# A deferred queue of small VectorE steps in an attention stage: weights, due steps, and the shift transposes one task step sooner

## The chip, the cores and the metric

The kernel runs on one core of one Trainium2 chip. The metric is the device time in microseconds (us) of one execution; lower is better. The core's engines each work through their own list of instructions in order and meet at semaphores: TensorE (PE in the profile, its weight loads PEld), VectorE (DVE), ScalarE (ACT), GpSimd (POOL), and SyncE (SP), which issues most DMAs.

## The reference

Two transformer layers on x of shape (2, 1024, 512), float32. Each layer is `x = x + layernorm(attn(layernorm(x)))` and then `x = x + layernorm(ffn(layernorm(x)))`. The first attention is a softmax over heads for every position on its own; the first feed-forward uses weights rounded to -1, 0, 1. The part that matters here is the second layer's attention, 16 query heads over 4 key heads of width 32, causal:

```
q, k, v = rope(x @ q_w.T), rope(k), v        # k, v from x @ kv_w.T
logits  = einsum('bhqd,bhkd->bhqk', q, k_ctx) / sqrt(32) + causal mask
probs   = softmax(logits, axis=-1)
out     = einsum('bhqk,bhkd->bhqd', probs, v_ctx)   # then @ c_w.T
```

The second feed-forward keeps the two largest of every four hidden values. Only the attention stage, from about 438 to 916 us of the profiled span, is touched by the change; the instructions of the other stages keep their order.

## The kernel before

The attention is cut into 16 tasks. A task is one batch b (0, 1), one block Q of 512 queries (0, 1) and one key head g (0 to 3), with the 4 query heads that share it; tiles carry these three numbers, so `mxs_0_1_2` belongs to batch 0, Q 1, g 2, which is task number 6 (`tk.n` runs 0 to 15 in that order). Each task is done twice over.

The first pass finds the softmax shift. `score_step` (L689 to L714) takes one tile of 128 queries and one chunk of up to 512 keys: for each head TensorE writes the scores into a PSUM bank (`psc`), VectorE takes the row maximum (`mxs`, L710), and ScalarE exponentiates in place and adds up the row (`psc`, L712, and `sms`). The bank is free once ScalarE is done with it. `shifts` (L974) then turns the maxima and sums into one number per row, maximum plus logarithm of the sum. For Q 1 it first merges two chunks: `mfin` and `md` on VectorE, an exponential of `md` on ScalarE (L986), then `md` times `sms` and `sfin` on VectorE. `minus_log` follows (tiles `lge` to `lgw`) and `in_pieces` splits the shift into three bf16 pieces in `pm0` or `pm1`. That is 23 small steps for Q 1, 18 for Q 0.

The second pass needs the shift along the other axis. `maxima_T` (L993) calls `pieces_T`: four TensorE transposes of the pieces (`pmt`, L927) into a bank and a VectorE copy to SBUF (`mT`, L929). `prob_step` then computes transposed scores (`pst`, L1004), adds the shift with a matmul against ones (`pst<-mT,onesb`, L1011), and ScalarE exponentiates into `pT` (L1017); `value_step` multiplies with v (`po`, L1033). Banks for `psc`, `pst`, `pmt`, projections and outputs come from one function, `ring`, which hands out seven PSUM banks in turn.

The main loop (L1283 on) runs over `t_steps`, one task step per 128 keys of a task's second pass. In each it issues a `prob_step`, then score steps of later tasks as far as `wanted(step)` asks (a step without any is called idle here), then some queued VectorE steps, then whatever `later` has put down for this step number. Projections of the second batch (`pq`, `pkv`, `ra` and `rbq`, `pkT`, `pqT`) and output products (`py`) are spread over the steps in this way.

The small VectorE steps are not issued where they are written. `shift_drops` and `norm_drops` are lists of calls: the first holds the shift steps, the second the inverse root (`nv_y`, `ny_y`, `rs_y`) and the four normalisations (`tmpy`, L237) of an output block. `drip(n)` takes n entries, shifts first. It is called with 2 after each row maximum, with 2 at the end of a step with scores and with 8 at the end of an idle step. Behind the exponential, `shifts` puts six empty entries, so that VectorE's next entry comes later than ScalarE's work. `apply` adds each normalised block to x on GpSimd (`x_sb`, L1063), which also finishes the rotations `ra` (L635).

```
shift_drops.items.append(lambda: nc.scalar.activation(d, d, AF.Exp))
shift_drops.items += [None] * 6
...
later(first[tk.n] - 1, [lambda: maxima_T(tk)])
...
n_drops = 2 if pos > before else 8
in_order(lambda: drip(n_drops))
```

`maxima_T` empties `shift_drops` first if anything is left. The order on VectorE is otherwise partly the scheduler's: in the built program the queued steps stand one after each maximum and the rest behind the last maximum of the step.

Of the kernel before, what the change touches and what calls it, by code (L numbers as in the profile page):

```python
# [13 lines left out]
AF = mybir.ActivationFunctionType  # L14
# [10 lines left out]
def two_layer_sandwich(  # L25
# [22 lines left out]
    nc = tc.nc  # L48
# [129 lines left out]
    class Drops:  # L178
# [1 line left out]
            self.items = []  # L180

        def __getattr__(self, op):
            return lambda *a, **kw: self.items.append(lambda: getattr(nc.vector, op)(*a, **kw))

        def drain(self, n=None):
            while self.items and n != 0:
                f = self.items.pop(0)
                if f is not None:
                    f()
                n = None if n is None else n - 1  # L190

    shift_drops, norm_drops = Drops(), Drops()

    def in_order(f):
        with tc.manual_schedule(engines={mybir.EngineType.DVE}):
            f()

    def drip(n):
        for _ in range(n):
            (shift_drops if shift_drops.items else norm_drops).drain(1)  # L200

    def ln_stats(pool, srcs, name, roots=True, st=None, vec=None):

# [32 lines left out]
    def ln_apply(dst, src, mv, rs, k, vec=None):  # L236
        (vec or nc.vector).tensor_scalar(  # L237
            dst, src, mv[:, k, 0:1], rs[:, k : k + 1], ALU.subtract, ALU.mult
        )
# [424 lines left out]
    for b in range(B):  # L664
        for Q in range(NQ):
            for g in range(NKV):
                tk = Task()
# [48 lines left out]
    with tc.manual_schedule(engines={mybir.EngineType.PE, mybir.EngineType.Pool}):  # L716
# [69 lines left out]
        for g in range(NG):  # L786
            nxt = None
            for hc in range(HC):
# [7 lines left out]
                if g == NG - 1 and hc == HC - 1:  # L796
                    tk = tasks[0]
# [38 lines left out]
                else:  # L836
# [10 lines left out]
                    elif hc == 2 * GT:  # L847
# [5 lines left out]
                        tk = tasks[0]  # L853
# [7 lines left out]
                step = HC * g + hc  # L861
# [49 lines left out]
    def in_pieces(m, name):  # L911

        nonlocal n_pm
        pm = pms[n_pm % 2]
        n_pm += 1
        r1 = s1.tile([P, GT, REP], F32, tag="r1", name=f"r1_{name}", bufs=1)
        shift_drops.tensor_copy(pm[:, :, :, 0], m)
        shift_drops.tensor_tensor(r1, m, pm[:, :, :, 0], ALU.subtract)
        shift_drops.tensor_copy(pm[:, :, :, 1], r1)
        shift_drops.tensor_tensor(pm[:, :, :, 2], r1, pm[:, :, :, 1], ALU.subtract)  # L920
        return pm
# [23 lines left out]
    def minus_log(v, m, name):  # L945


        def tmp(tag, dtype=F32):
            t = small_tile(tag, f"{tag}_{name}", dtype)
            return t.rearrange("p n k -> p (n k)")[:, : GT * REP].rearrange("p (i r) -> p i r", i=GT)  # L950

        vi = v.bitcast(I32)
        e, f = tmp("lge", I32), tmp("lgf", I32)
        ef, z, z2, p = tmp("lgw"), tmp("lgz"), tmp("lgy"), tmp("lgp")
        shift_drops.tensor_scalar(e, vi, 23, None, ALU.logical_shift_right)
        shift_drops.tensor_scalar(
            f, vi, 0x7FFFFF, 0x3F800000, ALU.bitwise_and, ALU.bitwise_or
        )
        fr = f.bitcast(F32)
        shift_drops.tensor_scalar(ef, e, -LN2, 126.5 * LN2, ALU.mult, ALU.add)  # L960
        shift_drops.tensor_scalar(z, fr, R2, None, ALU.add)
        shift_drops.reciprocal(z, z)
        shift_drops.scalar_tensor_tensor(z, fr, R2, z, ALU.subtract, ALU.mult)
        shift_drops.tensor_tensor(z2, z, z, ALU.mult)
        shift_drops.tensor_scalar(p, z2, 1.0 / 9.0, 1.0 / 7.0, ALU.mult, ALU.add)
        shift_drops.tensor_tensor(p, p, z2, ALU.mult)
        shift_drops.scalar_tensor_tensor(p, p, 1.0 / 5.0, z2, ALU.add, ALU.mult)
        shift_drops.scalar_tensor_tensor(p, p, 1.0 / 3.0, z2, ALU.add, ALU.mult)
        shift_drops.scalar_tensor_tensor(p, p, 1.0, z, ALU.add, ALU.mult)
        shift_drops.scalar_tensor_tensor(ef, p, -2.0, ef, ALU.mult, ALU.add)  # L970
        shift_drops.tensor_tensor(ef, ef, m, ALU.add)
        return ef

    def shifts(tk):  # L974

        in_order(shift_drops.drain)
        m, sm = tk.mx[:, :, :, 0], tk.sm[:, :, :, 0]
        if tk.Q > 0:
            n = tk.Q + 1
            m = s1.tile([P, GT, REP], F32, tag="mfin", name=f"mfin_{tk.nm}")  # L980
            shift_drops.tensor_reduce(m, tk.mx[:, :, :, :n], AX.X, ALU.min)
            d = s1.tile([P, GT, REP, n], F32, tag="md", name=f"md_{tk.nm}", bufs=1)
            shift_drops.tensor_tensor(
                d, m.unsqueeze(3).to_broadcast([P, GT, REP, n]), tk.mx[:, :, :, :n], ALU.subtract
            )
            shift_drops.items.append(lambda: nc.scalar.activation(d, d, AF.Exp))  # L986
            shift_drops.items += [None] * 6
            shift_drops.tensor_tensor(d, d, tk.sm[:, :, :, :n], ALU.mult)
            sm = s1.tile([P, GT, REP], F32, tag="sfin", name=f"sfin_{tk.nm}")
            shift_drops.tensor_reduce(sm, d, AX.X, ALU.add)  # L990
        tk.pm = in_pieces(minus_log(sm, m, tk.nm), tk.nm)

    def maxima_T(tk):  # L993
        in_order(shift_drops.drain)
        tk.mT = pieces_T(tk.pm, tk.nm)
# [47 lines left out]
    def output_parts(st, Q):  # L1043


        nm = f"y_{st.b}_{Q}"
        alone = st.b == B - 1 and Q == NQ - 1
        n = 1 if alone else GT
        ys = {}

        def y_of(ii):
            tag = "xn" if alone or ii == 0 else f"y{ii}"
            return s1.tile([P, D], F32, tag=tag, name=f"tmp{nm}_{ii}", bufs=1)

        def add(tiles, mv, ys):
            in_order(norm_drops.drain)
            vec = nc.vector if alone else norm_drops
            rs = inverse_root(s1, mv, n, f"{nm}_{tiles[0]}", vec=vec)

            def apply(k, ii):  # L1060
                ln_apply(ys[ii], py_of.pop(ii) if alone else ys[ii], mv, rs, k)
                xt = x_sb[:, st.b * TB + GT * Q + ii, :]
                soon(lambda: nc.gpsimd.tensor_tensor(xt, xt, ys[ii], ALU.add))  # L1063

            for k, ii in enumerate(tiles):
                if alone:
                    apply(k, ii)
                else:
                    norm_drops.items.append(lambda k=k, ii=ii: apply(k, ii))

        py_of, got = {}, []

        def part(ii):
            py = py_of[ii] = ring(f"p{nm}_{ii}")
            for c in range(DC):
                nc.tensor.matmul(  # L1076
                    py, st.oT[Q][:, c, ii * P : (ii + 1) * P], wc1[:, c, :],
                    start=(c == 0), stop=(c == DC - 1),
                )
            if ii == 0:  # L1080
                in_order(norm_drops.drain)
            ys[ii] = y_of(ii)
            if not got or alone:
                got[:] = [
                    s1.tile([P, n, 6], F32, tag=f"st_y{n}", name=f"st_{nm}_{ii}", bufs=1),
                    s1.tile([P, n, 2], F32, tag=f"mv_y{n}", name=f"mv_{nm}_{ii}", bufs=2),
                ]
            stats, mv = got
            k = 0 if alone else ii
            if not alone:  # L1090
                nc.vector.tensor_copy(ys[ii], py)
            nc.vector.bn_stats(out=stats[:, k, :], in_=py if alone else ys[ii])
            nc.vector.bn_aggr(out=mv[:, k, :], in_=stats[:, k, :])
            if alone:
                add([ii], mv, ys)

        parts = [lambda ii=ii: part(ii) for ii in range(GT)]
        return parts if alone else parts + [lambda: add(list(range(GT)), got[1], ys)]
# [6 lines left out]
    def later(step, parts, apart=1):  # L1105
        for k, f in enumerate(parts):
            due.setdefault(step + k * apart, []).append(f)
# [47 lines left out]
    with tc.manual_schedule(engines={mybir.EngineType.PE, mybir.EngineType.Pool}):  # L1155
# [2 lines left out]
            for tk in tasks for ii in range(GT) for ch in range(tk.Q + 1)  # L1158
        ]
        t_steps = [(tk, j) for tk in tasks for j in range(GT * tk.Q + GT)]  # L1160
        first, s_end, n = {}, {}, 0
        for tk in tasks:
            first[tk.n] = n
            n += GT * (tk.Q + 1)
# [1 line left out]
        pos = s_end[0]  # L1166

        def scored(tk):
            shifts(tk)
            later(first[tk.n] - 1, [lambda: maxima_T(tk)])  # L1170

        def scores_up_to(n, step, between=lambda: None):
            nonlocal pos
# [109 lines left out]
        for step, (tk, j) in enumerate(t_steps):  # L1283
            hold_adds[0] = True
            prob_step(tk, j)
            flush()
            prev.append((tk, j))

            waiting = [lambda: values(step)]

            def between():
                while waiting:
                    waiting.pop()()

            before = pos
            scores_up_to(wanted(step), step, between)
            between()
            n_drops = 2 if pos > before else 8
            in_order(lambda: drip(n_drops))
            for f in due.pop(step, []):  # L1300
                f()
        values(len(t_steps))
# [2 lines left out]
        while due:  # L1305
            step = min(due)
# [429 lines left out]
```

## Time and profile before

| | us |
|---|---|
| median of 3 runs | 1532.32 |
| the runs | 1530.01, 1533.43, 1532.32 |
| profiled execution, its own time | 1527.97 |
| profiled execution, span of its instructions | 1526.3 |
| TensorE busy | 1459.2 |
| VectorE busy | 1008.3 |
| ScalarE busy | 728.0 |
| GpSimd busy | 319.7 |

The profile is of one execution, 4.35 us shorter than the median of the timed runs, and 1.67 us of its time lie around the span. Busy times are sums over the whole span. A busy matmul can also be one that runs at a lower clock, so the granted clock has to be read beside it: its mean is 0.979 over the span, and the lower stretches are short and lie mostly in the attention stage.

### The profile page before, as it was taken

The page shows a single profiled execution, that of the slowest core. Times are in us where ns is not written, and L with a number is a line of the kernel's source. Part 1 is how long each engine was busy: PE and PEld are TensorE (multiplying, and loading weights), DVE is VectorE, ACT ScalarE, POOL GpSimd, SP SyncE. Part 2 cuts the span into 40 slices and gives each one's busy share as a digit, 9 for nine tenths or more (in the row PEclk, how much of TensorE's full clock was granted, in tenths as well). Part 3 has the DMA queues.
Part 4 walks back from the last instruction along what each step waited for, and adds up shares of the span by engine and source line. Part 5 has one row for each costly group of instructions (what it writes and reads, how often), then busy time and mean ns, then how long its engine had stood idle before and what let it go on. Part 6 is the DMA issues. An engine that isn't in the chain of part 4 may idle for free.

```text
span 1526.3 us, 20269 instructions
## 1 busy us (share of the span) xinstructions
PE 1459.2 (96%) x6998; PEld 1046.4 (69%) x6998; DVE 1008.3 (66%) x2315; ACT 728.0 (48%) x1847; POOL 319.7 (21%) x424
## 2 busy tenths in 40 slices
PE   7999999999889898999999999999999999999997
PEld 4558887767655454445444447888888888888886
DVE  6976465652577768657876645784688468846773
ACT  4243343322477656688886982450345034404420
POOL 1105475332222314323432011000200020001001
PEclk9999999999989999999999999999999999999998
DMA  7200211201474433343640003533452345235312
GB/s 296 76 14 28 83 56 42 56 18 53 107 176 108 118 100 90 102 127 92 175 135 1 1 1 145 205 133 145 171 195 97 145 172 201 92 149 212 147 49 76
DMA packets 78871, 167.52 MB, mean 110 GB/s; under 512 B 10224, under 2 KB 35824, under 8 KB 76720
## 3 DMA queue, kind: packets, MB, share of 16 engines
q1 hardware_dynamic: 72928, 148.39, 30.1%
q0 software_dynamic: 4784, 16.52, 2.8%
q10 hardware_dynamic: 1056, 1.31, 0.3%
q8 instruction: 55, 0.90, 0.2%
q14 instruction: 48, 0.39, 0.1%
HBM read 138.94 MB, written 27.26 MB: 109 GB/s over the span
## 4 chain that ended last, share of the span: by engine, by line
PE 80%; DVE 9%; ACT 6%; issue 2%; POOL 1%; DMA 1%; SPq 0%; DVEq 0%; ACTq 0%; POOLq 0%
PE acc L1496 13%; PE ph L409 9%; PE pb_u L1345 7%; PE pb_g L1345 7%; PE po L428 5%; PE py L1076 4%; PE pst L1004 4%; PE pq L286 4%; PE psc L698 4%; PE pc_u L1345 4%; PE pc_g L1345 4%; PE pq L603 4%; ACT psc L712 4%; PE po L1033 3%; DVE mxs L710 3%; PE pa_u L1345 2%
## 5 line engine op out<-in xcount | busy, mean ns | idle before, releaser
L710 DVE TENSOR_REDUCE mxs<-psc 128x1 f32<-128x512 f32 (+3 forms) x384 | 199.8, 550 | 70.7 <-PE psc L704 36.0
L712 ACT ACTIVATE psc<-psc,mxs 128x512 f32<-128x512 f32 (+3 forms) x384 | 217.5, 601 | 24.0 <-DVE mxs L710 18.1
L1017 ACT ACTIVATE pT<-pst 128x512 f32<-128x512 f32 (+3 forms) x384 | 160.2, 548 | 87.4 <-PE pst L1011 87.0
L409 PE MATMUL ph<-xTg,w 128*128 128x512 f32 x704 | 171.9, 397 | 1.7 <-DVE xTg L399 0.9
L409 PEld LDWEIGHTS ph<-xTg,w 128*128 128x128 f32 x704 | 132.1, 189 | 31.5 <-DVE xTg L399 1.2
L1549 POOL TENSOR_TENSOR x_sb<-x_sb,o 128x512 f32<-128x512 f32 x14 | 19.1, 1363 | 549.4 <-DVE o L237 549.2
L1496 PE MATMUL acc<-wd,h 128*128 128x256 f32 x512 | 121.6, 379 | 0.0
L1019 POOL TENSOR_SCALAR_AFFINE_SELECT pT<-pT 128x256 f32<-128x256 f32 x128 | 52.0, 413 | 309.3 <-ACT pT L1017 305.8
L1496 PEld LDWEIGHTS acc<-wd,h 128*128 128x128 f32 x512 | 97.0, 190 | 13.1
L712 ACT ACTIVATION_READ_ACCUMULATOR psc<-psc,mxs 128x1 f32 x384 | 96.0, 251 | 0.0
L1033 PE MATMUL po<-pT,v 128*32 128x512 f32 (+3 forms) x768 | 92.7, 520 | 1.5 <-POOL pT L1019 1.1
L1496 PE MATMUL acc<-wd,hx 128*128 128x256 f32 x384 | 93.3, 379 | 0.0
L698 PE MATMUL psc<-k,q 128*128 128x512 f32 (+3 forms) x256 | 90.9, 425 | 1.7 <-ACT psc L712 0.7
L418 POOL TENSOR_TENSOR hl<-h,hl 128x512 fp32r<-128x512 f32 x44 | 57.1, 1302 | 159.2 <-ACT hl L417 159.1
L428 PE MATMUL po<-w,hl 128*128 128x512 f32 x352 | 88.3, 393 | 0.4 <-DVE tmp L237 0.4
L1004 PE MATMUL pst<-q,k 128*128 128x512 f32 (+3 forms) x256 | 76.7, 394 | 11.5 <-ACT psc L712 10.8
L415 DVE TENSOR_TENSOR h<-h,ph 128x512 f32<-128x512 f32 x44 | 30.0, 684 | 83.9 <-PE ph L409 73.9
L1496 PEld LDWEIGHTS acc<-wd,hx 128*128 128x128 f32 x384 | 73.0, 190 | 9.9
L1406 DVE TENSOR_TENSOR gate<-gate,ab 128x1024 f32<-128x1024 f32 x32 | 39.2, 1225 | 59.2 <-ACT ab L1403 59.2
L698 PEld LDWEIGHTS psc<-k,q 128*128 128x128 f32 x256 | 49.0, 200 | 42.6 <-ACT pT L1017 18.6
L1513 ACT COPY p<-acc 128x512 f32<-128x512 f32 x8 | 4.7, 583 | 152.2 <-PE acc L1496 152.2
L428 PEld LDWEIGHTS po<-w,hl 128*128 128x128 f32 x352 | 65.7, 188 | 15.5 <-DVE tmp L237 1.3
(304 smaller groups left out, 3002.9 us busy)
## 6 DMA issues: line engine op xcount, KB each, us to landing
w<-kept SPq DMA_DIRECT2D x64, 512.0 KB, 5.8
wd<-keptd SPq DMA_DIRECT2D x16, 1024.0 KB, 7.8
q<-dq SPq DMA_DIRECT2D x60, 256.0 KB, 5.0
w<-in_f_wg SPq DMA_DIRECT2D x32, 384.0 KB, 3.5
w<-in_f_wu SPq DMA_DIRECT2D x32, 384.0 KB, 5.5
wd<-in_f_wd SPq DMA_DIRECT2D x16, 768.0 KB, 5.8
dq<-hl SPq DMA_DIRECT2D x32, 320.0 KB, 3.2
kept<-wl POOLq DMA_DIRECT2D x16, 512.0 KB, 3.0
```

The source lines that it names most:

```text
L286: nc.tensor.matmul(pa[:, :n], xT[:, c, :], w[:, c, :], start=(c == 0), stop=False)
L409: nc.tensor.matmul(pa, wt[:, c, cols], xT[:, s, c, :], start=(c == 0 and s == 0), stop=(c == DC - 1 and s == 1),)
L428: nc.tensor.matmul(pos0[g][k], hl[:, s, k * P : (k + 1) * P], w3[:, hc, :], start=(hc == 0 and s == 0), stop=(hc == HC - 1 and s == 1),)
L603: nc.tensor.matmul(pq, h.xT[:, c, :], wq1[:, c, :], start=(c == 0), stop=(c == DC - 1))
L698: nc.tensor.matmul(pa[:, :w], q.bitcast(F32R)[:, r, ii * P : (ii + 1) * P], k.bitcast(F32R)[:, g, :w], start=True, stop=True,)
L710: nc.vector.tensor_reduce(mx, pa[:, :w], AX.X, ALU.max, negate=True)
L712: nc.scalar.activation(pa[:, :w], pa[:, :w], AF.Exp, bias=mx, accum_out=tk.sm[:, ii, r, ch : ch + 1])
L1004: nc.tensor.matmul(pas[r][:, c0:], st.k[j // GT].bitcast(F32R)[:, g, (j % GT) * P : (j % GT + 1) * P], tk.q.bitcast(F32R)[:, r, c0:], star ...
L1017: nc.scalar.activation(p[:, e, c0:], pas[2 * pr + e][:, c0:], AF.Exp)
L1033: nc.tensor.matmul(tk.po[DK * r : DK * r + DK, c0:], st.v[j // GT][:, j % GT, g * DK : (g + 1) * DK], tk.pT[j, r // 2][:, r % 2, c0:], sta ...
L1345: nc.tensor.matmul(p, a[:, c, :], b[:, c, :], start=(first and c == 0), stop=(c == 1), skip_group_check=not first,)
L1496: nc.tensor.matmul(acc[m // 2][:, m % 2 * HW : (m % 2 + 1) * HW], a[:, j, k * P : (k + 1) * P], b[:, j, :], start=start, stop=True, skip_g ...
```

## The change

Every queue entry now has a cost: 4 for `bn_stats` and for the application of a normalisation, 1 for anything else. `drip` counts costs instead of entries, and always takes at least one entry when asked for any. It has two new arguments. With `upto` it goes on until no more than that many shift steps are left; the loop passes six times the number of steps still to go until `ready[0]`, which is two task steps ahead of the task's first `prob_step` for tasks 0 to 3, and three for the others. With `idle` it stops at an entry that is None. The six empty entries behind the exponential are gone. `maxima_T` is put down for two steps ahead of the task's first step instead of one, for tasks 4 to 15.

```diff
+            return lambda *a, **kw: self.put(
+                lambda: getattr(nc.vector, op)(*a, **kw), 4 if op == "bn_stats" else 1
+            )
+        def put(self, f, cost):
+            self.items.append((f, cost))
...
-    def drip(n):
-        for _ in range(n):
-            (shift_drops if shift_drops.items else norm_drops).drain(1)
+    def drip(n, idle=False, upto=None):
+        while n > 0 or (upto is not None and len(shift_drops.items) > upto):
+            q = shift_drops if shift_drops.items else norm_drops
+            if not q.items:
+                return
+            f, cost = q.items.pop(0)
+            n -= cost
+            if f is not None:
+                f()
+            elif idle:
+                while q.items and q.items[0][0] is None:
+                    q.items.pop(0)
+                return
...
         in_order(shift_drops.drain)
+        ready[0] = first[tk.n] - (2 if tk.n < 4 else 3)
...
-            shift_drops.items.append(lambda: nc.scalar.activation(d, d, AF.Exp))
-            shift_drops.items += [None] * 6
+            shift_drops.put(lambda: nc.scalar.activation(d, d, AF.Exp), 1)
...
-                    norm_drops.items.append(lambda k=k, ii=ii: apply(k, ii))
+                    norm_drops.put(lambda k=k, ii=ii: apply(k, ii), 4)
...
-            later(first[tk.n] - 1, [lambda: maxima_T(tk)])
+            later(first[tk.n] - (1 if tk.n < 4 else 2), [lambda: maxima_T(tk)])
...
-            n_drops = 2 if pos > before else 8
-            in_order(lambda: drip(n_drops))
+            idle, upto = pos == before, 6 * max(0, ready[0] - step)
+            in_order(lambda: drip(8 if idle else 2, idle, upto))
```

More of the change, by code (lines that the diff above doesn't have):

```diff
@@ L182, in __getattr__, with drain @@
         def __getattr__(self, op):
[L183 to L187, printed above, removed]
+            return lambda *a, **kw: self.put(
[3 more added lines that the diff above has]
+            self.items.append((f, cost))
+        def drain(self):
+            while self.items:
+                f, _ = self.items.pop(0)
                 if f is not None:
                     f()
-                n = None if n is None else n - 1
+    ready = [0]
+    first = {}
     shift_drops, norm_drops = Drops(), Drops()
@@ L1160, in two_layer_sandwich @@
         t_steps = [(tk, j) for tk in tasks for j in range(GT * tk.Q + GT)]
-        first, s_end, n = {}, {}, 0
+        s_end, n = {}, 0
         for tk in tasks:
```

## The prediction

> **What bounds the kernel now.** I read the page first, its busy times and its chain; then what TensorE waits for in the attention stage (435 to 920 us); then the timeline of each engine around the longest of these waits.
>
> ```profile
> PE 1459.2 (96%) x6998; PEld 1046.4 (69%) x6998; DVE 1008.3 (66%) x2315; ACT 728.0 (48%) x1847; POOL 319.7 (21%) x424
> ...
> PE 80%; DVE 9%; ACT 6%; issue 2%; POOL 1%; DMA 1%; SPq 0%; DVEq 0%; ACTq 0%; POOLq 0%
> ```
>
> TensorE is the bound of the whole, but 9% of the chain are VectorE's and 6% ScalarE's, and nearly all of that lies in the attention. There TensorE's waits are (in all, times, longest):
>
> ```profile
> PE pst L1004 <- ACT psc L712: 17.7, 43, 2.7
> ...
> PE pmt L927 <- DVE pm L183: 2.2, 2, 2.0
> PE pst L1011 <- DVE mT L929: 2.1, 4, 1.4
> ```
>
> The lower two lines, 4.3 us, are what an earlier transpose addresses directly; 0.5 us of them belong to tasks 2 and 3, which keep their place. The upper line is a bank that ScalarE has not freed. In most of the 43 ScalarE is itself busy without a gap, and no order on VectorE helps. In a few it waits for a row maximum that stands behind queued steps. The timeline shows where (start, length, and in brackets the wait before):
>
> ```profile
> 593.26 0.40 PE L1011 MATMUL pst<-mT,onesb 32*128 32x512 bf16 x4 [1.43 <-DVE mT L929]
> ...
> 598.38 0.95 PE L1004 MATMUL pst<-q,qk 128*128 128x512 f32 x2 [1.96 <-ACT psc L712]
> 599.77 0.74 PE L1004 MATMUL pst<-q,qk 128*128 128x512 f32 x1 [0.45 <-ACT psc L712]
> ...
> 636.87 0.68 PE L1004 MATMUL pst<-q,k 128*128 128x128 f32 x2 [1.30 <-ACT psc L712]
> ...
> 672.78 0.40 PE L927 MATMUL pmt<-identb,pm 128*128 128x128 bf16 x4 [2.02 <-DVE pm L183]
> ...
> 835.01 0.50 PE L1004 MATMUL pst<-q,k 128*128 128x512 f32 x1 [2.71 <-ACT psc L712]
> ```
>
> These six are 9.9 us of some 31 us of waits in the stage. Behind the waits at 598 and 835 stands the same thing, the four normalisations, with GpSimd's additions beside them; behind 636 a single shift step of 1.12 us between two maxima:
>
> ```profile
> 593.50 3.83 DVE L237 TENSOR_SCALAR tmpy<-tmpy,mv_y,rs_y 128x512 f32<-128x512 f32 x4
> ...
> 594.13 5.56 POOL L1063 TENSOR_TENSOR x_sb<-x_sb,tmpy 128x512 f32<-128x512 f32 x4 [2.62 <-DVE tmpy L237]
> ...
> 830.14 3.83 DVE L237 TENSOR_SCALAR tmpy<-tmpy,mv_y,rs_y 128x512 f32<-128x512 f32 x4
> ...
> 634.22 1.12 DVE L183 SCALAR_TENSOR_TENSOR lgp<-lgp,lgy 128x16 f32<-128x16 f32 x1
> ```
>
> The first two normalisations take 0.55 us, the next two 1.50, once GpSimd adds.
>
> **The change part by part.** No instruction is added or removed on any engine; the built program moves some 150 of VectorE's 2317, 12 of ScalarE's, 48 matmuls (the four `pmt` of each of tasks 4 to 15), two of GpSimd's and one DMA issue of SP's.
>
> (1) Batch 0, task 5 (`0_1_1`), 586 to 601. The rest of the shift now runs at 565 to 569, beside 2.5 and 4.3 us that VectorE waited for `py`. So the inverse root runs between the maxima at 580 to 584, three normalisations follow, and one remains, after the first maximum of the next score step. `pmt` goes ahead of the last `pst` of task 4, at about 587.9, and `mT` follows `rbk` at 588.7. The matmul against ones then starts when its `pst` are done, 591.65 instead of 593.26. The four `psc` behind it, though, now want banks of the step's maxima; these I put at 589.6, 591.6, 592.2 and 592.9 (the remaining normalisation at 1.3 us, blocked by GpSimd as in the row above), so `psc` goes out at 593.1 to 595.0, barely earlier. The gain comes behind it: no block of 3.83 us stands ahead of their maxima, ScalarE takes them at 596.0, right after its `pT`, instead of 597.76, and the ones matmul at 600.44 moves to 598.5. Gain 1.9 us. GpSimd's queue is the limit here: three additions of 1.45 us now stand ahead of the `ra` of the projection, which is done at 596.1 instead of 591.5, and `pqT` (595.58 before) waits for it 0.4 us. That is in the 1.9.
>
> (2) Task 6 (`0_1_2`), 621 to 643. The exponential now follows the last score at 621.7 instead of four `pT` later (623.61), so VectorE waits 0.8 us for it at once, with only `xT` behind it in its queue, which I put done at 625.0 to 625.5; `pq` wants it at 625.50. The shift is finished before the maxima at 632, so the 1.12 us step is gone from between them and ScalarE's scores end about 1 us sooner. Gain 0.8 us (0.3 to 1.6: the `pst` can't beat ScalarE).
>
> (3) Tasks 7 and 15 (`0_1_3`, `1_1_3`). The exponential comes 1.9 us earlier (665.43 to 663.5; four `pT` of 0.48 us), so the pieces are ready at 670.8 instead of 672.7. But `pmt` now stands ahead of 1.74 us of matmuls (669.02 to 670.76) that used to lie in the shadow of this chain. New wait 1.8 for the old 2.02: gain 0.25 us, and next to nothing in task 15.
>
> (4) Batch 1, task 13 (`1_1_1`), 824 to 836. Here all four normalisations move from behind the step's maxima to between the first and the second. I place them at 826.0, the last ending at 829.8, blocked as above. The second maximum then ends at 830.45 instead of 826.6, and TensorE waits 2.4 us at the next `psc` (829.0 to 831.4). The old wait of 2.71 at 835.01 shrinks: ScalarE reaches the score that frees that bank at 833.6 instead of 834.39. Gain 0.7 us, of two large numbers against each other (-1.1 to +2.7).
>
> (5) The four other waits for `mT` or `pm` from task 8 on (0.15, 0.14, 0.17, 0.23): gain 0.3 us.
>
> (6) Cost: `pmt` takes its bank eight times right behind a row of `psc`, so each following `pst` waits for one more score of ScalarE's, 0.35 us at 128 columns. Behind a ScalarE that is busy without a gap this costs nothing, and the later `pst` get it back; where that cover is missing it is 0.35 each, 2.8 in all. Taken at 0.8. The DMA issue moved is a store of `dq` ahead of a load of `q` that is first used 100 us later: nothing. Three `bn_stats` (0.67 us) move from 608 to 599, ahead of a store and of a maximum whose score ScalarE does not reach before: nothing.
>
> (7) The clock. Windows of the granted clock (last three columns: clock, DMA share, GB/s):
>
> ```profile
> 596.00:600.00 4.00, 1.59 (x6) 0.70 (x4) 4.00 (x9) 2.29 (x10) 4.00 (x4) 0.98 0.00 0
> 600.00:604.00 4.00, 4.00 (x16) 1.11 (x16) 2.53 (x5) 3.03 (x9) 3.11 (x5) 0.59 0.89 283
> 632.00:636.00 4.00, 3.07 (x22) 1.67 (x20) 3.92 (x9) 3.19 (x10) 3.14 (x5) 1.00 0.01 2
> 636.00:640.00 4.00, 3.11 (x17) 1.31 (x17) 3.10 (x14) 3.51 (x16) 1.32 (x3) 0.68 0.37 94
> ```
>
> After the waits of (1) and (2) the clock falls: 4 x 0.41 = 1.6 us and 4 x 0.32 = 1.3 us of TensorE time. The Trainium skill (TensorE: Matmul & The Clock Gate, Part 1: The HAM clock gate, and Why this matters for your kernels) has the clock drop after an idle window of about 3.4 us, and asks only for no gap above about 3 us. By that rule no wait here, 1.96 at most in (1) and (2), costs clock, and the sum ends without this term; the rows show the drop after windows merely 40% and 77% busy. I follow the rows, and take half of both, 1.4 us, since some waiting remains in either place.
>
> Sum: 1.9 + 0.8 + 0.25 + 0.7 + 0.3 - 0.8 + 1.4 = 4.6 us (3.2 by the skill's rule). The profiled execution's 1527.97 becomes 1523.4; against the median of the runs, 4.35 us above it, 1532.32 - 4.6 = 1527.7 us. About 0.2%, 3.1 us, is what a measurement of this kernel can tell from no change.
>
> **The rivals.** The first is that the change does not do what it says, and little comes of it. Nothing in the changed kernel puts a None into a queue any more, so the stop at ScalarE's wait never acts, and VectorE goes straight from `md` into waiting for the exponential. Where ScalarE is late by its `pT`, that wait was 3.49 us before already; for it speaks that (3) and (5) are small, and that in (1) GpSimd's `ra` limits what is won. If (1) gives half and the clock nothing: 0.95 + 0.8 + 0.25 + 0.3 - 0.8 = 1.5 us, 1530.8 us. Chance 0.28.
>
> The second ends slower: the normalisations between two maxima in (4). It decides if the second maximum of that step comes later than about 831.2, so that ScalarE, which has its scores, two `pT` and four more scores to do (4.9 us), reaches the bank later than before. If GpSimd blocks three of the four instead of two, or the maxima of both batches' steps wait this way, that is 0.95 us more each, the gains of (1) and (4) go (2.6), and two further half-clock windows are spent, 1.6 us each, on matmuls that are due. From +0: 2 x 0.95 + 3.2 + the 2.8 of (6) - 1.35 of the rest = 6.5 at most; half of that, 3.3, as the likely size: 1535.6 us. For it: the row 830.14 itself; against it: GpSimd stands idle from 826.3 to 830.77, so no more than two can be blocked if they start at 826. Chance 0.20.
>
> **How the numbers follow.** Forecast 0.52, first rival 0.28, slower 0.20. The forecast's own range is 1522.5 (both clock windows whole, (2) and (4) at their upper ends) to 1529.2. To hold 8 in 10 the range takes in the first rival and the lower part of the second: 1522.5 to 1536.5. Faster by over 0.2%: 0.52; within: 0.28; slower: 0.20.
>
> **What would show it.** In the changed profile: the ones matmul of task 5 without a wait for `mT`, and the wait of 1.96 behind it below 0.6; no wait above 0.7 in task 6's last `pst`; `pmt` of task 7 still waiting 1.5 to 2; a new wait of 2 to 3 at a `psc` of task 14's second score step; clock windows of 0.5 missing near 598 and 636. The forecast is wrong if ScalarE's wait for `mxs` grows from its 13.5 us, if a `tmpy` block of 3.8 us still stands ahead of maxima in batch 0, or if more windows run at half clock than before.

## The result and the profile after

The changed kernel takes 1528.01 us (median of 20 runs, 1522.91 to 1532.09) against 1533.93 us (20 runs) of the kernel before beside it: ratio 0.9958, interval 0.9947 to 0.9969. Measured a second time it was 1527.11 us (22 runs) against 1530.55 us (35 runs): 0.9983, interval 0.9972 to 0.9994. So it is faster, by 0.2 to 0.4%. The two intervals do not touch: between the two measurements the changed kernel's median differs by 0.9 us and that of the kernel before by 3.4, and why is open. The profiled execution took 1523.53 us, span 1521.8, 4.44 us less than the one before.

The busy times and the chain of the page:

```profile
PE 1458.7 (96%) x6998; PEld 1048.4 (69%) x6998; DVE 1005.5 (66%) x2315; ACT 728.2 (48%) x1847; POOL 320.1 (21%) x424
...
PE 80%; DVE 8%; ACT 7%; issue 2%; POOL 1%; DMA 0%; ACTq 0%; SPq 0%; DVEq 0%; POOLq 0%
```

No engine is busy for much less time (VectorE's 2.8 us are the most). What changed is when TensorE waits. Its waits in the attention stage (435 to 920 us; total, times, longest):

```profile
PE pst L1023 <- ACT psc L731: 10.5, 36, 0.8
PE psc L717 <- ACT pT L1036: 3.2, 5, 1.2
PE psc L717 <- ACT psc L731: 3.1, 9, 0.6
...
PE pmt L946 <- ACT psc L731: 1.3, 3, 0.7
...
PE pqT L537 <- POOL ra L654: 0.6, 1, 0.6
PE pmt L946 <- DVE pm L184: 0.6, 1, 0.6
PE pst L1030 <- DVE mT L948: 0.5, 2, 0.3
```

(Lines of the changed kernel lie some 19 lower: L1023 is the old L1004, L1030 the old L1011, L946 the old L927.) The first line was 17.7, longest 2.7; the last two were 2.2 and 2.1. Of the kinds shown, no wait above 1.23 us is left. The lines in the middle are new or larger (the two at `psc` were 1.6 and 1.7): nearly 5 us come back as waits at `psc`, `pmt` and `pqT`, most of them of half a microsecond.

The timeline at task 5, where the prediction's largest term lies (start, length, in brackets the wait before):

```profile
586.26 1.46 DVE L256 TENSOR_SCALAR tmpy<-tmpy,mv_y,rs_y 128x512 f32<-128x512 f32 x3
588.57 0.39 PE L946 MATMUL pmt<-identb,pm 128*128 128x128 bf16 x4
...
590.94 0.53 DVE L256 TENSOR_SCALAR tmpy<-tmpy,mv_y,rs_y 128x512 f32<-128x512 f32 x1
...
592.38 0.39 PE L1030 MATMUL pst<-mT,onesb 32*128 32x512 bf16 x4
...
596.08 0.49 ACT L731 ACTIVATE psc<-psc,mxs 128x256 f32<-128x256 f32 x1
...
596.78 0.66 PE L537 MATMUL pqT<-ident,ra 128*128 128x128 f32 x4 [0.58 <-POOL ra L654]
597.19 1.80 PE L1023 MATMUL pst<-q,qk 128*128 128x512 f32 x4
```

Three normalisations now stand ahead of the step, one behind its first maximum; the matmul against ones and the four `pst` at 597.19 have no wait in brackets, where 1.43 and 1.96 us stood. In their place `pkT` waits 0.61 us for a `pT` of ScalarE's at 595.89, and GpSimd's late `ra` holds `pqT` for 0.58.

To compare kernels I take from each trace TensorE's idle time between two matmuls that both have, and the length of the stretches there in which the trace has the granted clock at half (from the first `pst` of task 0 to the last `po` of task 15, 477 us):

| | length | TensorE idle | at half clock |
|---|---|---|---|
| before | 477.0 | 32.0 | 41.0 |
| changed | 471.6 | 27.2 | 41.0 |
| changed, second profile | 475.7 | 26.9 | 51.2 |

Between the two profiles of the changed kernel the idle time differs by 0.3 us and the half-clock time by 10, which is up to 5 us of TensorE's time; so the stage's 4.2 us of difference are not waits. In the two other programs profiled twice below, idle differed by 2.8 and 1.1 us, half-clock time by 17 and 0.

### The profile page after: what moved, and what is told of

It reads as the page before. It is cut to its first block, busy times and chain, and to the rows that moved or that the text cites. A ratio compares the mean times of both kernels' runs of the same rounds, so it can differ in the third digit from the quotient of the medians.

```text
span 1521.8 us, 20264 instructions
## 1 busy us (share of the span) xinstructions
PE 1458.7 (96%) x6998; PEld 1048.4 (69%) x6998; DVE 1005.5 (66%) x2315; ACT 728.2 (48%) x1847; POOL 320.1 (21%) x424
## 4 chain that ended last, share of the span: by engine, by line
PE 80%; DVE 8%; ACT 7%; issue 2%; POOL 1%; DMA 0%; ACTq 0%; SPq 0%; DVEq 0%; POOLq 0%
PE acc L1515 13%; PE ph L428 9%; PE pb_u L1364 7%; PE pb_g L1364 7%; PE po L447 4%; ACT psc L731 4%; PE psc L717 4%; PE pst L1023 4%; PE py L1095 4%; PE pc_u L1364 4%; PE pc_g L1364 4%; PE pq L622 4%; PE pq L305 4%; PE po L1052 3%; DVE mxs L729 3%; ACT pT L1036 2%
## 5 line engine op out<-in xcount | busy, mean ns | idle before, releaser
L1023 PE MATMUL pst<-q,k 128*128 128x512 f32 (+3 forms) x256 | 80.2, 408 | 7.6 <-ACT psc L731 6.3
```

What stands on the lines that cost most here:

```text
L1023: nc.tensor.matmul(pas[r][:, c0:], st.k[j // GT].bitcast(F32R)[:, g, (j % GT) * P : (j % GT + 1) * P], tk.q.bitcast(F32R)[:, r, c0:], star ...
```

## The experiments

All ratios are to the kernel before, run beside them. Idle is TensorE's in the stage, in us, from one profile. Clock is the mean granted clock over all the timed runs of a row; for the kernel before it was 0.9765, 0.9769 and 0.9771 beside the three rounds of experiments. A clock lower by 0.001 is up to 1.5 us of 1530.

| kernel | median us | ratio | interval | idle | clock |
|---|---|---|---|---|---|
| transposes sooner alone | 1541.20 | 1.0062 | 1.0045 to 1.0080 | 40.8 | 0.9732 |
| queue alone | 1525.32 | 0.9957 | 0.9943 to 0.9972 | 27.4 | 0.9784 |
| queue alone, again | 1525.56 | 0.9967 | 0.9952 to 0.9982 | 30.3 | 0.9780 |
| due steps alone | 1526.00 | 0.9971 | 0.9960 to 0.9983 | 26.8 | 0.9773 |
| due steps alone, again | 1525.42 | 0.9962 | 0.9950 to 0.9975 | 27.9 | 0.9775 |
| no empty entries, alone | 1528.94 | 0.9983 | 0.9972 to 0.9994 | 31.1 | 0.9778 |
| weights and no empty entries | 1530.12 | 0.9997 | 0.9987 to 1.0007 | 29.6 | 0.9771 |
| changed, without due steps | 1535.81 | 1.0022 | 1.0009 to 1.0035 | 34.6 | 0.9736 |
| changed, again | 1527.11 | 0.9983 | 0.9972 to 0.9994 | 26.9 | 0.9761 |
| sooner for tasks 5 and 13 only | 1525.93 | 0.9971 | 0.9961 to 0.9981 | 25.7 | 0.9762 |
| the same, normalisations at step ends | 1533.98 | 1.0022 | 1.0012 to 1.0033 | 33.7 | 0.9744 |
| sooner for task 13 only | 1525.23 | 0.9964 | 0.9950 to 0.9977 | 27.6 | 0.9782 |

**Transposes sooner alone**

```diff
-            later(first[tk.n] - 1, [lambda: maxima_T(tk)])
+            later(first[tk.n] - (1 if tk.n < 4 else 2), [lambda: maxima_T(tk)])
```

> The kernel before with one edit: the transposes of the shift pieces put down two steps ahead instead of one, for tasks 4 to 15; its queue is as it was. TensorE's order is then that of the changed kernel. Theory on record (the gain comes from what stands between row maxima on VectorE): the waits for mT and pm go (terms 3 and 5), but in tasks 5 and 13 the four normalisations now stand behind the first maximum of a row of four, so the waits of 2 to 2.7 us for a score bank stay. Gain 0 to 1.5 us, ratio to before 0.999 to 1.000. Rival (the sooner transposes alone make the gain): the whole 6 us, ratio 0.996. Third view (only the clock's low windows moved): number of windows below 0.8 in the stage falls in the same measure as the time.

Both expectations were wrong: it is 0.6% slower. TensorE's waits in the stage, and the one at task 6:

```profile
PE pmt L927 <- DVE pm L183: 13.7, 5, 3.6
PE pst L1004 <- ACT psc L712: 9.1, 28, 1.8
...
PE pmt L927 <- DVE nv_y L183: 2.5, 1, 2.5
...
639.11 0.18 DVE L183 TENSOR_TENSOR r<-lgw,pm 128x16 f32<-128x16 f32 x1
639.33 0.20 DVE L183 CAST pm<-r 128x16 bf16<-128x16 f32 x1
639.57 0.23 DVE L183 TENSOR_TENSOR pm<-r,pm 128x16 bf16<-128x16 f32 x1
639.85 0.61 PE L927 MATMUL pmt<-identb,pm 128*128 128x128 bf16 x4 [3.55 <-DVE pm L183]
```

The last piece is done at 639.80 and the transpose starts at once: the pieces are one step too late, in six of the twelve tasks, 16 us in all. The wait for a `pst` bank shrank, from 17.7 to 9.1 us, I take it because ScalarE goes on while TensorE stands at the pieces; idle time rose by 8.8 us net. The third view has a part in it: in the profile the stage spent 61.4 us at half clock instead of 41.0, and over all timed runs the clock was 0.0033 lower, up to 5 us of the 8.9.

**Changed, without due steps**

```diff
-            idle, upto = pos == before, 6 * max(0, ready[0] - step)
+            idle, upto = pos == before, None
```

> The changed kernel without the due steps: the queue is never driven beyond its quota of 2 or 8. Transposes sooner, weights of 4 and the missing empty entries stay. Theory on record: in tasks 5 the normalisations stand one behind each of the second to fourth maxima instead of ahead of the first, so term 1 loses about half (1 us), and the shift of tasks 6 is spread between the maxima again. Ratio to before 0.9965 to 0.9975. Rival (due steps are dead weight, since the transposes empty the queue anyway): as the changed kernel, 0.9955 to 0.996.

Both were wrong again in the same direction, and for the same reason, pieces that come too late:

```profile
PE pmt L946 <- DVE pm L184: 6.6, 3, 2.7
PE pmt L946 <- ACT psc L731: 5.2, 4, 2.6
```

Together 11.8 us, against 1.9 in the changed kernel. The second line names ScalarE, but at its two longest waits, at 780.75 and 864.62, the last piece too was done only 0.06 us before the transpose. Idle time is 2.6 us above that of the kernel before, and the clock over all runs 0.0029 lower, so part of the 3.5 us by which it is slower than that kernel is the clock's. The due steps are what lets the transposes stand a step sooner.

**Queue alone**, run twice

```diff
-        ready[0] = first[tk.n] - (2 if tk.n < 4 else 3)
+        ready[0] = first[tk.n] - 2
...
-            later(first[tk.n] - (1 if tk.n < 4 else 2), [lambda: maxima_T(tk)])
+            later(first[tk.n] - 1, [lambda: maxima_T(tk)])
```

> The changed kernel with the transposes put back to one step ahead, and the due step moved with them (two ahead for all tasks). TensorE's order is that of the kernel before. Theory on record: term 2 (0.8 us and its clock window, 1.3) and about half of term 1 (two normalisations stand ahead of the maxima of task 5's step, the others one behind each of two maxima) stay; the waits for mT and pm of 2.0 and some 1 us come back. Gain 2 to 3.5 us, ratio 0.9977 to 0.9987. Rival (the sooner transposes make the gain): ratio 0.999 to 1.001. In the profile: a wait of about 2 us for pm at task 7 in this kernel, 0.6 in the changed one.

> The changed kernel with the transposes one step ahead as before, once more, to stand beside the changed kernel on the same chip. Theory: ratio to before 0.9950 to 0.9970, within 1.5 us of the changed kernel. Rival (the sooner transposes are the gain with due steps): 2 us or more above the changed kernel.

The rival falls: the whole gain is there without the sooner transposes, and the first ratio lies below my range. The expected wait for `pm` at task 7 is not there (0.00, not 2): the pieces come early enough for a transpose at the old place. What is left is the copy `mT` of task 13 behind the four normalisations:

```profile
825.28 3.80 DVE L256 TENSOR_SCALAR tmpy<-tmpy,mv_y,rs_y 128x512 f32<-128x512 f32 x4
...
830.21 0.41 DVE L948 COPY mT<-pmt 128x512 bf16<-128x512 bf16 x1
830.66 0.62 PE L1030 MATMUL pst<-mT,onesb 32*128 32x512 bf16 x4 [3.88 <-DVE mT L948]
```

In the first profile of the same program that wait was 2.60: here a microsecond of difference comes from the execution alone.

**No empty entries alone**, and **weights and no empty entries**, without due steps

```diff
-            shift_drops.items += [None] * 6
```

> The kernel before without its six empty entries behind the exponential, nothing else. TensorE, ScalarE and GpSimd keep their order; 64 VectorE instructions move. Theory on record: the steps behind the exponential come earlier by six entries, so the normalisations of task 5 stand in pairs between maxima instead of four together, and the 1.12 us step of task 6 leaves the maxima. Gain 1 to 2.5 us, ratio 0.998 to 0.9993. Rival (the empty entries keep VectorE from waiting for ScalarE, so their loss costs): VectorE's waits for the exponential rise above the 12.8 us of before, ratio 1.001 or more.

The second kernel is the queue-alone kernel with `upto = None`.

> The changed kernel with two of its parts put back: transposes one step ahead as before, and no due steps. What stays of the change are the weights of 4 and the missing empty entries. Theory after the first four runs (the due steps make the gain): as the kernel without empty entries, ratio to before 0.998 to 1.000, and the 1.3 us wait at task 6 stays. Rival (weights and empty entries make it): 0.996.

Taking the empty entries away does no harm (VectorE waits 12.8 us for the exponential, as before), so that rival falls. What it gains is open: 0.9983 alone, 0.9997 together with the weights; and the 1.3 us wait at task 6 stays in both, as expected for the second kernel and against the expectation for the first. With the due steps in place the empty entries mean nothing: put back into the changed kernel, they leave every engine's instructions in the same order in the built program.

**Due steps alone**, run twice: the kernel before, entries counted one, empty entries kept

```diff
-    def drip(n):
-        for _ in range(n):
-            (shift_drops if shift_drops.items else norm_drops).drain(1)
+    def drip(n, upto=None):
+        while n > 0 or (upto is not None and len(shift_drops.items) > upto):
...
+        ready[0] = first[tk.n] - 2
...
+            upto = 6 * max(0, ready[0] - step)
+            in_order(lambda: drip(n_drops, upto))
```

> The kernel before with the due steps alone: entries all count one, the six empty entries stay, transposes stay one step ahead (due step two ahead). Five VectorE instructions stand elsewhere than in the kernel with the whole queue change. Theory (the due steps make the gain): ratio 0.9950 to 0.9965. Rival (the weights are needed): 0.998 or more.

> The kernel before with the due steps alone, once more beside the two others. Theory (the weights and the missing empty entries are worth nothing once there are due steps; five VectorE instructions differ): within 1 us of the queue-only kernel. Rival (the weights are worth what the first runs differed by): 2 us above it.

0.9971 (just outside the range) and 0.9962. TensorE's waits in the first profile:

```profile
PE pst L1012 <- ACT psc L719: 12.4, 41, 0.8
PE pst L1019 <- DVE mT L936: 3.4, 5, 2.6
```

The first was 17.7 in the kernel before, longest 2.7, and no wait for `pm` is left (2.2 before). VectorE, too, waits less for the exponential, 7.8 us instead of 12.8. Within the error this is the queue alone, so the due steps carry the gain, and the weights are worth nothing that shows.

**The changed kernel again**, on the same chip as the two "again" rows

> The changed kernel once more, beside the queue alone and the due steps alone on the same chip. Theory (with due steps the sooner transposes neither gain nor cost: they take away two waits for mT and bring waits of about 0.6 us at pmt): within 1.5 us of the queue-only kernel, ratio to before 0.9952 to 0.9970. Rival (the sooner transposes cost also with due steps): 2 us or more above the queue-only kernel.

1527.11 against 1525.56 and 1525.42 us: 1.6 and 1.7 us above, its ratio outside the expected range, with overlapping intervals. No gain of the sooner transposes shows once there are due steps; whether they cost 1 to 2 us is not settled, and with it whether the queue alone is the faster kernel. If they do, the record points at the clock and not at waits: the changed kernel has no more idle time than the queue alone, but a mean clock of 0.9769 and 0.9761 in its two measurements against 0.9784 and 0.9780.

**Sooner only where the copy stands behind a block**

```diff
+        ready[0] = first[tk.n] - (3 if tk.n in (5, 13) else 2)
...
+            later(first[tk.n] - (2 if tk.n in (5, 13) else 1), [lambda: maxima_T(tk)])
```

> The changed kernel with the sooner transposes for tasks 5 and 13 alone, the two whose copy mT stood behind the normalisations; the ten others go back to one step ahead, with their due step. Theory (a sooner transpose pays only where the copy stands behind a block, and elsewhere the matmul order makes TensorE wait 0.6 us for the pieces or the bank): the waits for mT of 1.05 and 2.60 us in the queue-only kernel go, those of about 0.6 at pmt of tasks 7 and 12 in the changed kernel go too. Stage 1 to 2 us shorter than either: ratio 0.9942 to 0.9955. Rival (the waits only change their name, for a score bank instead of mT): 0.9955 to 0.9965.

For task 13 alone, `(13,)` stands for `(5, 13)`:

> The changed kernel with the sooner transposes for task 13 alone, where the queue-only kernel still waits 2.60 us for mT; all others one step ahead with their due step. Theory (a sooner transpose pays where the copy stands behind a block of normalisations, and only there): the wait of 2.60 becomes one of about 1.2 at a score bank, the rest is the queue-only kernel; idle time of the stage 25 to 26.5 us, ratio to before 0.9950 to 0.9965, at or 1.5 us below the queue-only kernel. Rival (what is won there is given back in half-clock stretches): equal to the queue-only kernel within 1 us.

In the second kernel the copy goes ahead of the block, and the wait moves to a score bank:

```profile
824.31 3.93 DVE L256 TENSOR_SCALAR tmpy<-tmpy,mv_y,rs_y 128x512 f32<-128x512 f32 x4
...
827.55 0.39 PE L1030 MATMUL pst<-mT,onesb 32*128 32x512 bf16 x4
829.17 0.39 PE L717 MATMUL psc<-k,q 128*128 128x256 f32 x1 [1.23 <-ACT pT L1036]
```

As expected at this place, 2.60 became 1.23; no wait for the pieces is left at tasks 7 and 12 in either, and the two-task kernel has the least idle time of all, 25.7 us. In time neither is clearly below the queue alone: the two-task kernel's ratio lies above what either theory gave, the other's (with more idle than expected, 27.6) fits both. A microsecond of idle is less than what the clock does between executions. No version tried here is shown to beat the changed kernel.

**The same two, normalisations only at the ends of steps**

```diff
-                drip(2)
+                if shift_drops.items:
+                    drip(2)
```

> As the kernel with two tasks sooner, and after a row maximum only shift steps are taken, so that the inverse root and the normalisations stand at the ends of steps: in task 5 all four ahead of the copy mT, in task 13 three right after mT and one four maxima later. Theory (the block between two maxima is what delays TensorE there, 1.2 us): that wait goes, ratio 0.9935 to 0.995. Rival (the last normalisation and so GpSimd's addition come ahead of ra, and TensorE waits for pqT longer than the 0.6 us of the changed kernel): at or above the kernel with two tasks sooner.

Slower by 0.5% than the kernel it was made from; neither theory named why. The 1.2 us wait did go, but elsewhere inverse root and normalisation now pile up at the end of a step, and the first maximum of the next stands behind all of them:

```profile
739.13 0.66 DVE L184 SCALAR_TENSOR_TENSOR rs_y<-nv_y,rs_y 128x4 f32<-128x4 f32 x1
739.83 0.55 DVE L256 TENSOR_SCALAR tmpy<-tmpy,mv_y,rs_y 128x512 f32<-128x512 f32 x1
740.29 0.68 DVE L729 TENSOR_REDUCE mxs<-psc 128x1 f32<-128x512 f32 x1
...
741.90 0.33 PE L717 MATMUL psc<-k,q 128*128 128x128 f32 x1 [2.56 <-ACT psc L732]
```

The longest wait of this kernel, 3.62 us at 780.10, stands behind shift steps that take up to 1.22 us each beside GpSimd's additions (rows from just before it stand in the last section). So here the same steps cost more gathered ahead of the maxima than one by one between them.

## Why the prediction was right or wrong

The forecast of 1527.7 us stood against 1528.01, and its difference of 4.6 us lies between the two measured, 5.9 (1533.93 - 1528.01) and 3.4. By its terms, the two numbers being the first and second profile of the changed kernel:

(1) Task 5, 1.9 us: right in mechanism, a little small. TensorE's idle time from the seventh step of task 4 to the third of task 5 fell from 4.12 to 1.74 and 1.73 us. ScalarE takes the scores right after its `pT`, as forecast; at 596.08 that looks like the 596.0 of the forecast, but this execution runs 0.9 us late there (`pkv` starts at 586.85, not 585.96), so it is 0.8 sooner. `pqT` waits 0.58 for `ra` (0.4).

(2) Task 6, 0.8 us: right; idle over the last two steps of task 5 and the first of task 6 fell from 1.99 to 1.43 and 1.05. The longest wait at its last `pst` is 0.34.

(3) Task 7, 0.25 us: wrong in size. The wait for `pm` is 0.58 and 0.32, not 1.8:

```profile
659.46 0.54 ACT L1006 ACTIVATE md<-md 128x32 f32<-128x32 f32 x1
660.03 0.19 DVE L184 TENSOR_TENSOR md<-md,sms 128x32 f32<-128x32 f32 x1 [1.56 <-ACT md L1006]
...
665.24 0.47 DVE L184 TENSOR_TENSOR pm<-r,pm 128x16 bf16<-128x16 f32 x1
665.77 0.40 PE L946 MATMUL pmt<-identb,pm 128*128 128x128 bf16 x4 [0.58 <-DVE pm L184]
```

VectorE's wait for the exponential fell from 3.49 to 1.56, the 1.9 that I had counted. But from the product `md` to the last piece it took 5.7 us (660.03 to 665.71) instead of 6.7 (665.99 to 672.73), which I had taken over unchanged: a chain of small steps has no fixed length. So the term was 1.4 to 1.7 us at the wait, and came from the queue; the sooner transpose alone made the 0.58.

(4) Task 13, 0.7 us: the new wait is 1.23 rather than 2.4, the old 2.71 is gone, and idle went from 3.51 to 2.75, but to 3.68 in the second profile, where 1.03 us follow two matmuls later. Gain 0.8, or a loss of 0.2: inside the bounds that I gave, and no better known than that.

(5) and (6), together a cost of 0.5: idle of tasks 7 (after its first step) to 12 rose by 0.35 and 0.9 us. About right, though these steps hold other waits as well.

(7) The clock, 1.4 us: wrong. Rows of the same form as in the prediction, of the changed kernel:

```profile
596.00:600.00 4.00, 3.42 (x14) 1.75 (x13) 3.05 (x10) 3.08 (x12) 3.68 (x5) 0.69 0.02 4
...
636.00:640.00 4.00, 3.80 (x26) 2.09 (x25) 2.50 (x6) 3.81 (x13) 3.58 (x7) 1.00 0.82 236
688.00:692.00 4.00, 3.34 (x24) 2.05 (x20) 3.53 (x13) 2.90 (x15) 1.61 (x4) 1.00 0.00 0
692.00:696.00 4.00, 4.00 (x25) 2.06 (x22) 1.90 (x4) 3.33 (x13) 1.51 (x3) 0.63 0.01 2
```

and of its second profile, near the same matmuls as the row at 636:

```profile
630.00:634.00 4.00, 3.30 (x19) 1.56 (x18) 2.36 (x8) 3.41 (x17) 2.16 (x5) 0.70 0.30 71
634.00:638.00 4.00, 4.00 (x15) 2.80 (x11) 1.85 (x5) 3.15 (x10) 3.60 (x6) 0.50 0.66 195
```

The low stretch near 598 stayed, the one near 637 went in one execution and not in the other, and others came, as at 692. The sum, 41.0 us, is that of before, and 51.2 in the second. The timed runs agree that nothing came back: their mean clock is 0.9765 over 42 of the changed kernel and 0.9768 over 116 of the kernel before. The skill's rule that the prediction quotes had put the term at nothing, which was the better number, though its condition does not describe these rows: they are low with no gap near 3 us. That the total was right all the same is in part luck, two errors against each other: the waits fell by 4.9 and 5.1 us where terms (1) to (6) said 3.2 (1.0 of the 5.1 lies ahead of the seventh step of task 4, where no term stands), and the clock gave back nothing where I took 1.4.

Two of the signs named for a wrong forecast came true in the second profile and not in the first: more half-clock time, and 15.8 us of ScalarE's wait for `mxs` instead of 13.5 (12.8 in the first). They lie within what one program does between executions and could not decide. The lower end of the forecast's range, 1522.5, is not the sum of the terms named for it, which give 1523.5; and the first rival's sum leaves out term (4) without saying why.

The first rival had its fact right, that the stop at an empty entry never acts, and its conclusion wrong: 1.5 us of gain against 3.4 and 5.9. The due steps do the work, and I had not named them as the carrier. The second rival's block between two maxima is there, at 1.23 us instead of the 2.4 that the prediction priced, and does not decide. A slower end did exist, in none of my cases: the sooner transposes without pieces ready for them.

## What to carry to other kernels

Give a deferred queue a due date: what gained here is that the steps on the way to a waited-for result are forced out before their consumer is due, while steps without such a consumer may trail behind. No run raised the quota of 2 by itself, so whether a higher rate would have done as well is not shown. Moving the consumer earlier gained nothing that shows, and where the producer wasn't moved first it cost 16 us of waits, of which 8.9 us were left in the time; so when a change does both, run each alone, because the sum can hide a part that loses. And forecast waits, with an uncertainty for the clock: the idle time of one program differed between two profiles by 0.3 to 2.8 us, its half-clock time by up to 17.

## What the hardware showed

The granted clock falls without a long gap. Over the 14 profiles, cut into the 3.41 us stretches in which the clock changes, and counting only stretches between 432 and 920 us that themselves run at full clock, the next stretch was at half clock in 49 of 49 cases where TensorE had been busy below 60% by the trace, in 36 of 51 at 60 to 70%, 51 of 113 at 70 to 80%, 7 of 194 at 80 to 90%, and in none of some 1390 above. Of the 143 stretches ahead of a half-clock one, 92 met no wait of 1 us or more, and 5 met one above 3. The changed kernel's two profiles, 0.3 us apart in idle time, had 12 and 15 half-clock stretches; I take it that the stretches fall differently on the waits in each execution.

A step of 0.16 us can take 1.2 beside GpSimd. The same operation in the changed kernel, and in the kernel with the normalisations at the ends of steps, there with an addition of GpSimd's:

```profile
623.59 0.16 DVE L184 SCALAR_TENSOR_TENSOR lgp<-lgp,lgz 128x16 f32<-128x16 f32 x1
```

```profile
773.41 2.52 POOL L1083 TENSOR_TENSOR x_sb<-x_sb,tmpy 128x512 f32<-128x512 f32 x2
773.50 1.22 DVE L184 SCALAR_TENSOR_TENSOR lgp<-lgp,lgz 128x16 f32<-128x16 f32 x1
774.76 1.20 DVE L184 SCALAR_TENSOR_TENSOR lgw<-lgp,lgw 128x16 f32<-128x16 f32 x1
```

Two additions take 2.52 us, and each small step ends about when one of them does. The Trainium skill (SBUF — State Buffer, SBUF: two separate sides) has the two engines share a pair of ports that one holds for its whole instruction, and the rows agree. It is what I take to have made the chain of term (3) 5.7 us in one kernel and 6.7 in the other: in the slower chain three steps of 0.64 to 0.66 us (at 668.03, 670.14 and 671.58) end within 0.06 us after a `wr` step of GpSimd's, in the faster one two do (0.67 at 662.48, 0.70 at 664.05). No run tested that by itself.
